# Tangent sums to rows: a product with a centring matrix, in two parts, in place of transposes and a row mean

## The chip, the cores and the metric

The kernel runs on one core of a Trainium2 chip. The metric is the device time of one execution in microseconds (us), given as the median of several runs. Below, PE is TensorE, DVE is VectorE, ACT is ScalarE, POOL is GpSimd, and SP is the engine whose queue issues the loads.

## What is computed

Four graph layers run one after the other on x (4096 rows of 64) and a dense 0/1 matrix adj (4096 by 4096, fp32). Each is followed by a residual and a layer norm. Layer 0 is a mean over neighbours with a linear map, layer 2 a weighted sum over the last 100 neighbours, and layers 1 and 3 are hyperbolic attention. Of these, layer 3 cut to its core (layer 1 is alike but for constants):

```
x_tan = _logmap0(x)
x_local = _logmap(x[:, None, :], x[None, :, :])
logits = (x_tan @ w_l)[:, None] + (x_tan @ w_r)[None, :] + att_b[0]
adj_att = sigmoid(logits) * adj
support_t = einsum('ij,ijd->id', adj_att, x_local)
return _proj(_expmap(x, support_t))
```

The kernel never forms x_local. For a row i the sum over j comes out as a combination of x_i and of sums over j of a weight times a row that depends on j alone. These last sums are the "tangent sums" of this document. The rows that go into them carry a multiple of their scale in every one of their 64 columns, so that the sum of a result row over its 64 columns gives the total weight, and the row less its own mean gives the part along the x_j.

## The kernel before

**Tiling.** 4096 rows are 32 blocks of 128 (`NB`), and 4 groups of 1024 (`NW`, `GROUPS`, taken from 3 down to 0). A group is eight blocks (`WB`). Every pass over adj goes group by group; within a group, 16 loads `g` of 1 MB bring two blocks each.

**Attention (`attend`, L914).** For each of the two blocks of a load, PE makes scores `zp` for 1024 columns (L935, L938, L941), ACT makes `sig` (L943) and `sq` (L946), DVE multiplies (L949), then once for both blocks DVE does L951, and PE adds up into `acc` (L955). After 16 loads ACT copies `acc` to `sums` (L962): 128 partitions by 512 columns. The 128 partitions are two halves of 64 features, the first for the group's rows 0 to 511, the second for rows 512 to 1023.

**Moving the rows (`move`, L972).** For each group, `move` turns `sums` to rows (`to_rows_of`: four fp32 PE transposes, L969, into one PSUM tile `aux`), ACT copies them to `of` (the buffer named `z0`, L985), DVE sums each row (`sum_1`, L988), divides by 64 (L989), and subtracts the mean, which gives `u` (L991). POOL multiplies x by `u` (L992), ACT squares `u` (L994), and DVE sums both over the row (L999, L997). Then follows a chain of some fifty DVE operations on 128 by 8 numbers (L1001 to L1065, with three reciprocal square roots of ten operations each, L673 to L679), and at the end `u` and x are scaled (L1068, and L1067 on POOL) and added to give the next layer's rows (L1071). In layer 3, `store` writes these rows out (L1407, issued from ACT's queue); after layer 1, `linear` turns them into the supports of layer 2 (L1081 to L1103).

**What sets the order.** `move`, `linear`, `prepare` and `store` are generators: each `yield n` hands back the turn for n ticks, and the passes call `tick` once or more for every block. `near()`, `soon()` and `after(n)` give such waits; in layers 1 and 3 each of them is one tick, in layer 2 `near()` is one, `soon()` none and `after(12)` three. The main queue takes `behind` of the group before and then `move` of this group. So the `move` of a group runs during the pass of the next group; that of group 0 of layer 1 runs during the first pass of layer 2, and that of group 0 of layer 3 after all passes. The program order so made is then list-scheduled, with each engine running its own list in order, except in layers 0 and 2, where the order on PE and ACT stays as written (`manual_schedule`, `FIXED`).

**Buffers.** `take` hands out one of two PSUM tiles named `aux` (one bank each), shared by `move`, `linear`, `prepare` and `spread_left`; `free` makes a generator wait in program order while one is in use. Tiles from `grp` and `nums` have one buffer for each name: a second `move` can write `u` only when L1071 of the first has read it.

Of the kernel before, what the change touches and what calls it, by code (L numbers as in the profile page):

```python
# [10 lines left out]
F32 = mybir.dt.float32  # L11
# [4 lines left out]
ALU = mybir.AluOpType  # L16
AX = mybir.AxisListType
PSUM = bass.MemoryType.PSUM

P = 128  # L20
N = 4096
D = 64
# [9 lines left out]
WB = WW // P  # L32
# [26 lines left out]
def gnn_stack_kernel(  # L59
# [15 lines left out]
    nc = tc.nc  # L75
    V = nc.vector
# [3 lines left out]
    ident = const.tile([P, P], F32, name="ident")  # L80
# [488 lines left out]
    def stream(fits):  # L569

        with ExitStack() as st:

            def pool(name, bufs=1, **kw):
                return st.enter_context(tc.tile_pool(name=name, bufs=bufs, **kw))

            keep = pool("f_keep")
            xs = pool("f_xs", 2)
            loads = pool("f_loads", 6)
            row = pool("f_row")
# [10 lines left out]
            queues, place, done, held = ([], []), [0, 0], set(), []  # L590
# [27 lines left out]
            def soon():  # L618


                return 0 if place[0] in (0, 2) else 1

            def after(small):


                each = {0: 1.6, 2: 6.0}.get(place[0])
                return 1 if each is None else 1 + int(small / each)

            def near():

                return 3 if place[0] == 0 else 1

            def take(dtype, *shape):

                held.append(1)
                return aux.tile(list(shape), dtype, name="aux")

            def free():
                while held:
                    yield 1  # L640
# [3 lines left out]
            def x_of(layer):  # L644

                if layer not in layers_x:
                    layers_x[layer] = xs.tile([P, NB, D], F32, name="x")
                return layers_x[layer]
# [10 lines left out]
            def grp(name, bufs=None):  # L659
                kw = {"bufs": bufs} if bufs else {}  # L660
                return row.tile([P, WB, D], F32, name=name, **kw)

            def nums(name, n=WB):
                return row.tile([P, n], F32, name=name)

            def over(v):
                return v[:, :, None].to_broadcast([P, v.shape[1], D])
# [29 lines left out]
            V.memset(turn, ROOT + OFF)  # L697

            ys = keep.tile([P, WB, 3 * D + 10], F16, name="ys")
            yd = keep.tile([P, WB, D + 10], F16, name="yd")
# [2 lines left out]
            for k in range(3):  # L705
                part = float(np.float16(rest))
# [258 lines left out]
            def to_rows_of(sums):  # L965

                t = take(F32, P, SB, 2, D)
                for k in range(SB):
                    nc.tensor.transpose(t[:, k], sums[:, k * P : (k + 1) * P], ident)  # L969
                return t.rearrange("p k h f -> p h k f")  # L970

            def move(layer, s, sums, curve):  # L972
# [4 lines left out]
                least = 1e-15 if layer == 1 else 1e-30  # L977
                at = blocks(s)
                xg, x2g = x_of(layer)[:, at, :], x2[:, at]
                sum_1, k, d, uu = nums("sum_1"), nums("k"), nums("d"), nums("uu")  # L980
                u, w, sq, of = grp("u"), grp("w_att"), grp("sq"), grp("z0")
                yield from free()
                t = to_rows_of(sums)
                yield near()
                nc.scalar.copy(of.rearrange("p (h k) f -> p h k f", h=2), t)  # L985
                held.pop()
                yield near()
                V.tensor_reduce(sum_1, of, AX.X, ALU.add)  # L988
                V.tensor_scalar(k, sum_1, 1.0 / D, None, ALU.mult)  # L989
                yield soon()  # L990
                V.tensor_sub(u, of, over(k))  # L991
                nc.gpsimd.tensor_mul(w, xg, u)  # L992
                yield after(12)
                nc.scalar.activation(sq, u, AF.Square)  # L994
                yield near()
                yield soon()
# [27 lines left out]
                y2, xy, den, p, q = (nums(n) for n in ("y2", "xy", "den", "p", "q"))  # L1024
# [16 lines left out]
                px, qd, w2, t = nums("px"), nums("qd"), nums("w2"), nums("mt")  # L1041
# [85 lines left out]
            with ExitStack() as lp:  # L1127
# [85 lines left out]
                with tc.manual_schedule(engines=FIXED):  # L1213
                    for s in GROUPS:
                        sums = [ps.tile([P, W], F32, name="acc") for _ in range(2)]
                        counts = [ps.tile([P, W], F32, name="acc") for _ in range(2)]
                        parts = ((first, sums, P), (third, counts, D + 1))
                        for g in reversed(range(NB // 2)):
# [5 lines left out]
                            for k in (1, 0):  # L1224
                                j = 2 * g + k
                                for lhs, accs, m in parts:
                                    for h in range(2):
# [3 lines left out]
                                            start=j == BLOCKS[0], stop=j == BLOCKS[-1],  # L1231
                                        )
                            if g == s * WB // 2 + 1:

                                for lhs, accs, m in parts:
                                    for h in range(2):
                                        for k in range(SB):
# [3 lines left out]
                                                start=False, stop=False,  # L1241
# [24 lines left out]
            def attention(layer, curve, rates, behind):  # L1266

                need((layer, GROUPS[0]))
                for n, s in enumerate(GROUPS):
                    if n:  # L1270
                        need((layer, s, "left"))
                    then = GROUPS[n + 1] if n + 1 < NW else None
                    sums = attend(layer, s, rates[n], then)
                    move_s = move(layer, s, sums, curve)
                    if n:
                        last = n + 1 == NW
                        later(in_turn((layer + 1, s + 1), behind(s + 1)), last, 9 * last)
                    later(move_s)
                    if n + 1 == NW:
                        later(in_turn((layer + 1, s), behind(s)))  # L1280
# [113 lines left out]
            with tc.manual_schedule(engines=FIXED):  # L1394

                for some in (GROUPS[:2], GROUPS[2:3], GROUPS[3:]):
                    accs = wide_pass(some) if len(some) == 2 else narrow_pass(some[0])
                    for s, acc in zip(some, accs):
                        sums = row.tile([P, W], F32, name="sums", bufs=2)
# [15 lines left out]
            t, g = nums("m1", 1), nums("g1", 1)  # L1415
# [4 lines left out]
            sq = row.tile([P, D], F32, name="w_sq")  # L1420
# [16 lines left out]

    fits = const.tile([P, 1], F32, name="fits")
    stream(fits)

    n_fit = const.tile([1, 1], I32, name="n_fit")
    with tc.tile_pool(name="fit_ps", bufs=1, space=PSUM) as ps:
        t = ps.tile([1, P], F32, name="fit_t")
# [52 lines left out]
```

## Time and profile before

| | |
|---|---|
| median of 3 runs | 1151.56 us (1148.69 to 1153.72) |
| the profiled execution | 1150.32 us, span 1148.8 us |
| PE, DVE, ACT, POOL busy | 1012.6, 964.3, 820.6, 60.3 us |
| granted PE clock, mean | 0.969 |
| HBM read | 269.55 MB, 236 GB/s over the span |
| attention groups of layer 1 (copies of `sums`) | 281.3, 364.4, 451.0, 539.2 us |
| attention groups of layer 3 (copies of `sums`) | 868.2, 951.5, 1033.8, 1114.7 us |
| passes of layer 2 (first copy of their sums) | 643.3, 706.1, 777.1 us |

The span is the time from the first to the last instruction in the profile of one execution; the time of that execution is 1.5 us longer. The copies of `sums` mark the ends of the groups, so that one reads off how long a group lasts: 82.3 us from 951.5 to 1033.8. The busy time of PE is modelled from the starts of its matmuls, so a PE that is 88% busy isn't at 88% of its peak. A mean over the span hides stages with different limits: the document goes by stage.

### The profile page before, as it was taken

The numbers are of one execution on the slowest core, as the hardware profiler recorded it, in microseconds if no ns is written. First come the engines' busy times: TensorE is split into PE (matmuls) and PEld (weight loads), VectorE is DVE, ScalarE is ACT, GpSimd is POOL, SyncE is SP. The second block draws the span as 40 slices with busy tenths as digits, with TensorE's granted clock in tenths as the row PEclk, the third lists the DMA queues.
The fourth block names the chain that finished last, engine by engine and source line by source line (L and its number), as shares of the span: only waits on it lengthen the run. The fifth ranks groups of instructions, "written<-read, shape, count | busy, mean of one in ns | idle before, by whom it ended". The sixth has DMA issues, their size and how long they took to land.

```text
span 1148.8 us, 13484 instructions
## 1 busy us (share of the span) xinstructions
PE 1012.6 (88%) x4832; PEld 386.9 (34%) x4917; DVE 964.3 (84%) x1901; ACT 820.6 (71%) x886; POOL 60.3 (5%) x97
## 2 busy tenths in 40 slices
PE   6999897899899999988999987898898999999870
PEld 3445544233333333332333232233333333233320
DVE  5687898999999899989773476529998999999996
ACT  0003215899889788976767778888998998889850
POOL 0020120000000000000000020000000000000001
PEclk9999998999999999999999999899999999999995
DMA  9999998556566466644988976686465666566400
GB/s 344 421 381 400 373 417 329 193 176 218 176 210 218 164 209 210 220 169 140 323 297 312 341 268 235 220 278 235 150 217 183 220 218 204 204 210 206 149 1 21
DMA packets 38418, 271.57 MB, mean 236 GB/s; under 512 B 4550, under 2 KB 4550, under 8 KB 5574
## 3 DMA queue, kind: packets, MB, share of 16 engines
q1 hardware_dynamic: 37440, 269.50, 65.3%
q10 hardware_dynamic: 902, 1.12, 0.3%
q8 instruction: 40, 0.66, 0.2%
q14 instruction: 36, 0.29, 0.1%
HBM read 269.55 MB, written 1.05 MB: 236 GB/s over the span
## 4 chain that ended last, share of the span: by engine, by line
DVE 57%; PE 26%; ACT 7%; DMA 4%; issue 3%; POOL 2%; SPq 0%; ACTq 0%; POOLq 0%
DVE t L951 20%; DVE t L949 20%; PE z L1372 8%; PE acc L1387 5%; PE acc L955 4%; DMA edges<-in_adj_dram 4%; PE acc L1229 3%; DVE junk L741 2%; ACT sq L946 2%; ACT sq L1381 2%; PE z L935 1%; PE z L938 1%; POOL sq L768 1%; PE aux L842 1%; PE z L941 1%
## 5 line engine op out<-in xcount | busy, mean ns | idle before, releaser
L943 ACT ACTIVATE sig<-left_b,right 128x1024 f32<-128x1024 f32 x256 | 293.8, 1149 | 45.9 <-DVE t L949 35.0
L949 DVE SCALAR_TENSOR_TENSOR t<-z,sig 128x1024 f32<-128x1024 f32 x256 | 309.9, 1216 | 13.9 <-ACT sq L946 12.9
L946 ACT ACTIVATE sq<-z,turn 128x1024 f32<-128x1024 f32 x256 | 281.5, 1106 | 27.3 <-PE z L941 25.1
L951 DVE SCALAR_TENSOR_TENSOR t<-sq,t 128x2048 f32<-128x2048 f32 x128 | 292.9, 2289 | 0.7
L955 PE MATMUL acc<-t,xe 128*64 128x512 f32 x1024 | 260.2, 619 | 32.3 <-DVE t L951 28.7
L935 PE MATMUL z<-edges,two_i 128*128 128x512 bf16 x465 | 183.1, 394 | 19.7 <-DVE t L949 19.5
L938 PE MATMUL z<-lo_hi,hi_lo 128*128 128x512 f16 x512 | 194.1, 379 | 3.2
L941 PE MATMUL z<-dst,src 74*128 74x512 f16 x512 | 195.1, 381 | 0.0
L1381 ACT ACTIVATE sq<-z,at_edge 128x512 bf16<-128x512 f32 (+1 forms) x192 | 152.6, 829 | 51.3 <-PE z L1372 47.9
L955 PEld LDWEIGHTS acc<-t,xe 128*64 128x64 f32 x1024 | 64.0, 138 | 168.5 <-DVE t L951 88.4
L741 DVE SCALAR_TENSOR_TENSOR t<-edges 128x2048 bf16<-128x2048 f32 x32 | 73.9, 2311 | 38.5 <-DMA edges<-in_adj_dram 37.5
L1372 PE MATMUL z<-edges,pass_by 128*128 128x512 bf16 x241 | 87.5, 400 | 17.3 <-ACT sq L1381 15.8
L935 PEld LDWEIGHTS <-two_i 128*128 128x128 bf16 x512 | 50.3, 98 | 142.7 <-issue 97.7
L1229 PE MATMUL acc<-edges,first 128*128 128x512 bf16 x241 | 77.4, 397 | 21.4 <-DMA edges<-in_adj_dram 20.7
L1387 PE MATMUL acc<-sq,halves 128*64 128x512 bf16 x512 | 82.0, 398 | 5.7 <-ACT sq L1381 3.5
L1372 PE MATMUL z<-edges,enter 128*128 128x512 bf16 x240 | 85.1, 397 | 0.1
L1229 PE MATMUL acc<-edges,third 128*65 128x512 bf16 x256 | 80.9, 398 | 0.6
L741 DVE SCALAR_TENSOR_TENSOR junk<-edges 128x2048 bf16<-128x2048 f32 x32 | 73.2, 2286 | 5.1 <-DMA edges<-in_adj_dram 4.8
L938 PEld LDWEIGHTS <-hi_lo 128*128 128x128 f16 x512 | 50.3, 98 | 67.9 <-issue 23.7
L941 PEld LDWEIGHTS <-src 74*128 74x128 f16 x512 | 49.4, 96 | 69.2 <-issue 4.0
L1229 PEld LDWEIGHTS <-first 128*128 128x128 bf16 x256 | 24.3, 98 | 50.2 <-issue 22.6
L1387 PEld LDWEIGHTS <-halves 128*64 128x64 f16 x512 | 18.9, 108 | 63.0 <-issue 62.7
(260 smaller groups left out, 758.3 us busy)
## 6 DMA issues: line engine op xcount, KB each, us to landing
edges<-in_adj_dram SPq DMA_DIRECT2D x256, 1024.0 KB, 4.9
x<-in_x_dram SPq DMA_DIRECT2D x4, 256.0 KB
out_dram<-x ACTq DMA_DIRECT2D x4, 256.0 KB, 4.0
w_sb<-in_L_gnn_W_dram ACTq DMA_DIRECT2D x1, 32.0 KB, 4.8
given<-in_L_gnn_b_dram ACTq DMA_DIRECT2D x1, 0.2 KB
given<-in_L_gnn_bias_dram ACTq DMA_DIRECT2D x1, 0.2 KB
given<-in_L_gnn_b_att_dram ACTq DMA_DIRECT2D x1, 0.0 KB
given<-in_L_gnn_att_b_dram ACTq DMA_DIRECT2D x1, 0.0 KB
```

What stands on the lines that cost most here:

```text
L741: V.scalar_tensor_tensor(junk, a, 0.0, a, ALU.not_equal, ALU.not_equal, accum_out=odd[:, n : n + 1])
L935: nc.tensor.matmul(half, two_i, edge[:, at : at + W], start=True, stop=False)
L938: nc.tensor.matmul(half, hi_lo[:, of], lo_hi[:, to], start=False, stop=False)
L941: nc.tensor.matmul(half, src[:, of], dst[:, to], start=False, stop=True)
L943: nc.scalar.activation(sig, left_b, AF.Sigmoid, bias=right[:, j : j + 1])
L946: nc.scalar.activation(sq[:, k], zp, AF.Square, bias=turn, scale=-1.0 / UNIT)
L949: V.scalar_tensor_tensor(t[:, k], zp, 0.0, sig, ALU.max, ALU.mult)
L951: V.scalar_tensor_tensor(t, sq, HIGH**2, t, ALU.add, ALU.mult)
L955: nc.tensor.matmul(acc[h * D : (h + 1) * D, :], xe[:, j, :], t[:, k, h * W : (h + 1) * W], start=j == BLOCKS[0], stop=j == BLOCKS[-1],)
L1229: nc.tensor.matmul(accs[h][:m], lhs[:, j, :], edge[:, at : at + W], start=j == BLOCKS[0], stop=j == BLOCKS[-1],)
L1372: nc.tensor.matmul(z[:, h : h + W], lhs, rhs[:, h : h + W], start=j == BLOCKS[0], stop=True, skip_group_check=True,)
L1381: nc.scalar.activation(w, z[:, :n], AF.Exp, bias=at_edge, scale=-LN2)
```

## The change

A constant `centre` (128 by 2 by 65) is made once. For half h, its rows h*64 to h*64+63 hold, in columns 0 to 63, the identity less 1/64, and in column 64 ones; all else is zero. A product of 128 columns of `sums` (as the stationary operand) with `centre` gives, for 128 rows of each half, the row less its mean and, in the 65th column, its sum. Four such products make a group. Each has 2 x 65 = 130 output columns[...]: they are done in two parts of two, each with its own `aux` tile and its own ACT copy. The copies write `all_u` (named `u_1`, 65 columns a row), of which `u` and `sum_1` are now views. The transposes, the copy to `of`, the row sum, the division and the subtraction are gone from `move`, and one `yield after(12)` ahead of the square. `to_rows_of` stays in use in `end_2`.

```diff
@@ setup @@
+            centre = keep.tile([P, 2, D + 1], F32, name="centre")
+            V.memset(centre, 0.0)
+            for h in range(2):
+                of = slice(h * D, (h + 1) * D)
+                V.tensor_scalar(
+                    centre[of, h, :D], ident[of, of], -1.0 / D, None, ALU.add
+                )
+                V.memset(centre[of, h, D:], 1.0)
@@ move @@
-                sum_1, k, d, uu = nums("sum_1"), nums("k"), nums("d"), nums("uu")
-                u, w, sq, of = grp("u"), grp("w_att"), grp("sq"), grp("z0")
-                yield from free()
-                t = to_rows_of(sums)
-                yield near()
-                nc.scalar.copy(of.rearrange("p (h k) f -> p h k f", h=2), t)
-                held.pop()
-                yield near()
-                V.tensor_reduce(sum_1, of, AX.X, ALU.add)
-                V.tensor_scalar(k, sum_1, 1.0 / D, None, ALU.mult)
-                yield soon()
-                V.tensor_sub(u, of, over(k))
+                k, d, uu = nums("k"), nums("d"), nums("uu")
+                w, sq = grp("w_att"), grp("sq")
+
+                all_u = row.tile([P, WB, D + 1], F32, name="u_1")
+                u, sum_1 = all_u[:, :, :D], all_u[:, :, D]
+                for part in range(2):
+                    yield from free()
+                    t = take(F32, P, 2, 2, D + 1)
+                    for i in range(2):
+                        cols = slice((2 * part + i) * P, (2 * part + i + 1) * P)
+                        nc.tensor.matmul(t[:, i], sums[:, cols], centre, start=True, stop=True)
+                    yield near()
+                    nc.scalar.copy(
+                        all_u.rearrange("p (h k) f -> p k h f", h=2)[:, 2 * part : 2 * part + 2], t
+                    )
+                    held.pop()
+                    yield near()
                 nc.gpsimd.tensor_mul(w, xg, u)
-                yield after(12)
                 nc.scalar.activation(sq, u, AF.Square)
                 yield near()
                 yield soon()
```

## The prediction

> **What bounds the kernel now.** I read the chain of work that ended last first, then engine busy time by stage, then the operations that the change touches, then DVE's timeline where they stand, and the table of waits.
>
> ```profile
> DVE 57%; PE 26%; ACT 7%; DMA 4%; issue 3%; POOL 2%; SPq 0%; ACTq 0%; POOLq 0%
> ...
> 540.00:645.00 105.00, 101.70 (x539) 33.84 (x548) 59.40 (x175) 73.19 (x76) 4.41 (x3) 1.00 0.85 301
> ...
> 952.00:1034.00 82.00, 76.99 (x326) 26.57 (x330) 80.57 (x116) 72.04 (x71) 2.32 (x2) 0.98 0.61 207
> ...
> 1115.00:1149.00 34.00, 0.93 (x5) 0.50 (x5) 21.04 (x116) 1.72 (x4) 4.38 (x3) 0.55 0.05 19
> ```
>
> The columns of a stretch are its length, then busy us of PE, weight loads, DVE, ACT, POOL. In an attention group of layer 3 (952 to 1034) DVE is busy 80.57 of 82.00 us: it is the bound, and PE (76.99) is close. In the first pass of layer 2 (540 to 645) PE is busy 101.70 of 105.00 and DVE is not the bound. From 1115 on only one chain of small DVE operations is left.
>
> ```profile
> L985 ACT COPY z<-aux x8: 572/574/586, 282.8 to 1116.0; 128x512 f32<-128x512 f32 x8
> ...
> L988 DVE TENSOR_REDUCE sum<-z x8: 676/678/686, 283.8 to 1116.7; 128x8 f32<-128x512 f32 x8
> ...
> L991 DVE TENSOR_TENSOR u<-z,k x8: 679/686/694, 285.7 to 1124.3; 128x512 f32<-128x512 f32 x8
> ...
> L969 PE MATMUL aux<-ident,sums x48: 270/273/329, 282.0 to 1115.7; 128*128 128x128 f32 x48
> ...
> L992 POOL TENSOR_TENSOR w_att<-x,u x8: 1263/1276/1284, 286.5 to 1125.1; 128x512 f32<-128x512 f32 x8
> ```
>
> Eight moves, one for each group of two layers. Their start times give the places: six lie inside attention groups (283, 397, 503, 871, 954 and 1036 us), one in layer 2 (559), one in the tail (1117). Of the 48 transposes 32 are the moves'; `end_2` keeps 16.
>
> ```profile
> 974.36 0.68 DVE L1071 TENSOR_TENSOR x<-u,w_att 128x512 f32<-128x512 f32 x1
> 974.96 1.22 DVE L949 SCALAR_TENSOR_TENSOR t<-z,sig 128x1024 f32<-128x1024 f32 x1
> 976.09 0.68 DVE L991 TENSOR_TENSOR u<-z,k 128x512 f32<-128x512 f32 x1
> 976.69 1.22 DVE L949 SCALAR_TENSOR_TENSOR t<-z,sig 128x1024 f32<-128x1024 f32 x1
> ...
> 1115.65 0.17 DVE L677 TENSOR_TENSOR rs_t<-n 128x8 f32<-128x8 f32 x1
> 1116.65 0.69 DVE L988 TENSOR_REDUCE sum<-z 128x8 f32<-128x512 f32 x1 [0.83 <-ACT z L985]
> 1117.26 0.16 DVE L678 SCALAR_TENSOR_TENSOR rs_t<-rs_t,mt 128x8 f32<-128x8 f32 x1
> ...
> 1123.54 0.69 DVE L1071 TENSOR_TENSOR x<-u,w_att 128x512 f32<-128x512 f32 x1 [0.93 <-POOL w_att L1067]
> 1124.26 0.69 DVE L991 TENSOR_TENSOR u<-z,k 128x512 f32<-128x512 f32 x1
> ```
>
> Two things to see. In the loop L991 takes 0.60 us of DVE, start to start. And `u` has one buffer: L991 of a move runs only after L1071 of the move before it, although its L988 ran long before (954 against 976; 1116.65 against 1124.26). In the tail L988 sits in the middle of the older move's square root and holds it from 1115.82 to 1117.26.
>
> ```profile
> DVE d L999 <- POOL w_att L992: 8.6, 6, 1.5
> ...
> ACT sq L994 <- DVE u L991: 9.2, 2, 8.4
> ```
>
> After L991, DVE stands still for POOL's product, about 1.4 us in six of the eight moves (four of them in the loop).
>
> **What the Trainium skill says.** (1) FP8 and Floating Point Precision, TensorE Precision Notes: a true fp32 product takes four passes. The trace agrees: the fp32 products of L1186 and L1187, 65 columns each, stand 0.111 us apart (two records, 0.056 us each), and 4 x 65 columns at the 2.4 GHz that TensorE: Matmul & The Clock Gate gives in its opening table are 0.108. (2) SBUF — State Buffer, Who interferes with whom: a DVE instruction with two SBUF inputs and a GpSimd instruction that reads SBUF block each other for a whole instruction. It agrees: POOL's L768 takes 1.04 us alone and 2.95 to 3.11 beside DVE's L741. (3) VectorE: DVE Perf Modes, Mode 1×: this mode asks nothing of strides. So a `u` with rows 65 apart should cost L1068 and L1071 nothing; no row before shows it.
>
> **The change, part by part.**
>
> *Removed from DVE.* L988 (0.60 us start to start), L989 (0.08 to 0.17; I take 0.10) and L991 (0.60): 1.30 us a move. In the six loop moves that is work of the bound engine: 6 x 1.30 = 7.8 us gained. In layer 2 PE is the bound: nothing.
>
> *PE.* Four transposes (0.11 us apart, 0.44 in all) become four fp32 products of 130 columns: twice L1186's 0.111 us, 0.22 each, 0.89 in all, 0.45 more a move. Lower end: nothing more; upper end: 0.96 more, if each part also shows the 0.27 us of a lone matmul. What hides it: late in an attention group the scores of the second block are ready at 1097.14 (end of L941) and DVE takes them at 1098.33, 1.2 us later. That cover is good in the dense groups of layer 3 (moves at 954 and 1036). At the other four group changes DVE does wait for ACT's L946 and that for PE's L941 (1.45 us at 299.03, 2.37 at 394.54, 2.39 at 506.39), so I charge 4 x 0.45 = 1.8 us. Without any cover it would be 2.7.
>
> *ACT.* One copy of 512 columns (0.574) becomes two of 260. The nearest row, L1102 with 256 columns out of PSUM, takes 0.379: 0.76, or 0.19 more. ACT is busy 72.04 of 82.00 us there; I charge nothing (1.1 us over six moves without cover).
>
> *Ticks.* In layers 1 and 3 the square (L994) stays four ticks after the start (two `near`, `soon`, `after` against four `near`). In layer 2 it comes after four instead of five.
>
> *Wait moved to ACT.* The copies now write the single `u_1` themselves, so ACT, no longer DVE, waits for L1071 of the move before. Behind them on ACT stand the next L943 and L946, and DVE waits for those. In the loop of layer 3 the copies must lie about 975 and 1076, where ACT has gaps (1.17 us before 976.21); I take nothing. Both `aux` buffers are held meanwhile (952 to 975), so `spread_left` (L910 at 960) moves to about 977; it is needed at 1034. In layer 2, where ACT's order is written out, L985 ran at 555.58, but L1071 ends at 556.88: with the copy (0.38) the next L1381 starts about 1.1 us late, and PE behind it about 1.0. In exchange ACT's 0.82 us wait for L991 goes, which had cost PE 0.60. With PE's own 0.45: a loss of 0.9 us.
>
> *POOL.* L992 now waits for ACT; POOL has nothing queued behind. DVE no longer stops for it right after L991, so the four 1.4 us stalls in the loop can vanish (5.6 gained); or L992 collides with L951, which has two SBUF inputs, and holds it 1.3 us (4 x 1.3 = 5.2 lost). I take a quarter of the gain, 1.4 us.
>
> *Tail.* The stall at L988 goes: 1.44 us, and 0.1 for L989. After L1071 (end 1124.23) POOL started at 1125.10; now two copies of 0.38, overlapping by about 0.09, and a handover: about 0.80 instead of 0.87. 1.5 us gained. If the store's DMA issue (0.34 on ACT) goes ahead of them, 1.2.
>
> *Set-up.* Five small DVE operations for `centre`, 0.06 to 0.22 each as their like at 0.9 to 9.3 us, in all about 0.6: DVE waits 2.67 us for the first x there. Nothing; 0.6 without that cover. SP's loads are not touched, and DMA is at 0.61 in these groups.
>
> *Sum:* -7.8 + 1.8 + 0.9 - 1.4 - 1.5 = -8.0 us. Against the profiled execution, 1150.32 us (span 1148.8 and 1.5 around it), that is 1142.3; this execution is 1.24 below the median of 1151.56, so for the median 1143.5.
>
> **Rivals.**
>
> *Half the gain.* The group changes are bound by PE and ACT, not DVE. For it: the waits named at 299, 394 and 506. Then only the two dense moves and the tail count: -2.6 - 1.5 + 0.9 = -3.2, about 1148.4. Against it: even those stretches begin with DVE operations in a row.
>
> *More than forecast.* All four POOL stalls vanish, 4.2 us beyond the quarter taken: 1139.3. For it: the two dense moves (L991 at 976 and 1077) have other work ahead of L999 and no stall already. Against it: L951 next to L992.
>
> *Slower.* ACT is stopped in order by the single `u_1`. If, in layer 3, the copies stand one pair of blocks too early in ACT's queue, ACT is held a full cycle (4.75 us, L951 to L951) and the pipeline then refills (PE's scores 2.64 and L946 1.11): 8.5 us at each of two places, 17 us, 1160.5. It decides from some 14 us of such ACT waits on. For it: ACT did wait for DVE in order in layer 2 and the tail (L994, L1020). Against it: no such wait in the loop.
>
> **How the numbers follow.** Forecast 0.58 (1139 to 1147.5, of which 0.10 above 1145.8); half the gain 0.20; more 0.10; slower 0.12 (0.10 beyond 1157.3). 0.5%, 5.8 us, is about what a measurement of this kernel can tell from no change. So faster 0.58, same 0.32, slower 0.10. Leaving out the far half of the low case and the slower one, the range is 1138 to 1154.
>
> **What would show it.** Right: DVE's busy time in a layer 3 group down by about 1.3 and the group shorter by as much; ACT copies waiting for L1071 only in layer 2 (about 1.3 us) and the tail; no L988 in the tail, and a tail 1.5 us shorter; PE records of the product 0.11 us apart. Wrong: DVE less busy with the group as long (PE or ACT bound), L951 above 2.29 us beside L992, or ACT idle before the copies in the loop.

## The result, and the profile after

The changed kernel takes 1143.13 us (median of 15 runs, 1137.66 to 1148.34), the kernel before, run beside it, 1151.75 us (15 runs, 1147.20 to 1154.66). The ratio is 0.9923, with a 95% interval of 0.9907 to 0.9939: 0.8% faster, 8.6 us between the medians. The prediction was 1143.5. The profiled execution takes 1140.81 us, with a span of 1139.1 (before: 1150.32 and 1148.8).

The total came as forecast. The places did not. Lines have moved by 10 to 14: L949 and L951 are now L959 and L961, L946 is L956, the product is L1000 and its copies L1002, POOL's product L1007, the row sums L1011 and L1013, the end of a move L1079 to L1085. The table gives the time from one copy of `sums` to the next.

| us | before | after | difference | predicted, about |
|---|---|---|---|---|
| layer 1, three groups with a move | 83.1, 86.6, 88.2 | 81.2, 86.3, 86.9 | -3.5 | -3.6 |
| layer 2, first pass | 104.1 | 104.0 | -0.1 | +0.9 |
| layer 3, three groups with a move | 83.3, 82.3, 80.9 | 81.2, 81.1, 84.6 | +0.4 | -3.8 |
| tail | 34.1 | 26.0 | -8.1 | -1.5 |

The last column puts the terms of the prediction where they belong: a loop move is 1.30 us off DVE, and in the four that aren't in the dense groups 0.35 us of stalls goes and 0.45 us of PE comes. The rows add up to -11.3 us, the span to -9.7: the other +1.6 lies in layer 0 with the first group of layer 1, the last two passes of layer 2 and the first group of layer 3, which differ by 1 to 3 us (the first of them by up to 5) between kernels with the same code there.

The chain of work that ended last, of the changed kernel:

```profile
DVE 53%; PE 29%; ACT 8%; DMA 6%; POOL 2%; issue 2%; ACTq 0%; SPq 0%; POOLq 0%; DVEq 0%
```

DVE's share is down from 57% and PE's is up from 26%. The next view is the busy time by stretch, of the three groups of layer 3 and the tail (its columns as in the prediction; the number in brackets counts instructions, and the last three columns are the granted PE clock, the share of DMA and GB/s):

```profile
866.20:947.40 81.20, 77.08 (x338) 26.92 (x336) 79.82 (x119) 72.74 (x72) 1.31 (x1) 1.00 0.61 208
947.40:1028.50 81.10, 77.01 (x338) 26.96 (x336) 79.97 (x114) 72.70 (x73) 4.88 (x2) 1.00 0.62 211
1028.50:1113.10 84.60, 76.16 (x318) 25.49 (x315) 82.71 (x147) 66.67 (x66) 3.07 (x2) 0.96 0.35 122
1113.10:1139.10 26.00, 1.50 (x9) 1.05 (x9) 15.88 (x87) 2.05 (x5) 4.29 (x3) 0.57 0.07 24
```

The same stretches before:

```profile
868.20:951.50 83.30, 77.93 (x329) 26.87 (x334) 80.23 (x115) 72.86 (x72) 1.27 (x1) 0.98 0.60 204
951.50:1033.80 82.30, 77.29 (x327) 26.67 (x331) 80.87 (x116) 72.34 (x71) 2.32 (x2) 0.98 0.61 207
1033.80:1114.70 80.90, 73.44 (x308) 24.72 (x311) 80.59 (x131) 66.41 (x64) 2.32 (x2) 0.98 0.37 127
1114.70:1148.80 34.10, 0.93 (x5) 0.50 (x5) 21.31 (x117) 2.01 (x4) 4.38 (x3) 0.55 0.05 19
```

A move has three DVE instructions fewer, yet two of the three groups have more of them than before (119 and 147), and the tail has 30 fewer. Work has changed place. Over these four stretches DVE is busy 258.4 us instead of 263.0 and idle 14.5 instead of 17.6: of the 7.7 us that layer 3 gains, 4.6 are DVE's work and 3.1 its idle time. In the three groups of layer 1 DVE is busy 1.1 us more than before (245.9 against 244.8), since operations have come in there too (the first pass of layer 2 has 141 DVE instructions instead of 175); the 3.5 us gained are idle time alone.

The operations concerned, and two lines from the table of waits (total us, times, longest):

```profile
L1002 ACT COPY u<-aux x16: 358/378/382, 281.4 to 1116.4; 128x260 f32<-128x260 f32 x16
L1007 POOL TENSOR_TENSOR w_att<-x,u x8: 1178/1306/3324, 282.2 to 1116.9; 128x512 f32<-128x512 f32 x8
...
L1085 DVE TENSOR_TENSOR x<-u,w_att x8: 675/686/693, 371.4 to 1133.8; 128x512 f32<-128x512 f32 x8
```

```profile
DVE d L1013 <- POOL w_att L1007: 7.3, 5, 3.5
...
ACT u L1002 <- DVE x L1085: 3.4, 2, 2.5
```

The copies take the 0.38 us expected, and `u` in rows 65 apart costs L1085 nothing (0.686 against 0.683 us for L1071). ACT waits for L1085 twice, 2.5 us in the tail and 0.9 inside the second group of layer 3:

```profile
954.74 0.66 ACT L1002 COPY u<-aux 128x260 f32<-128x260 f32 x2 [0.87 <-DVE x L1085]
```

In layer 2 it doesn't wait for L1085, which starts there at 544.7, six us ahead of the first copy (550.74). DVE still stands still for POOL's product, 7.3 us in all. In the six attention groups with a move that wait is 5.7 us before and after. What has gone there is DVE's waits for ACT's scores (`sq`, L946): 9.0 us before, 1.2 after.

Now the start of a group of layer 3, DVE's timeline (start, duration):

```profile
869.85 0.69 DVE L1013 TENSOR_REDUCE d<-w_att 128x8 f32<-128x512 f32 x1 [1.07 <-POOL w_att L1007]
870.45 1.22 DVE L959 SCALAR_TENSOR_TENSOR t<-z,sig 128x1024 f32<-128x1024 f32 x1
871.58 0.68 DVE L1011 TENSOR_REDUCE uu<-sq 128x8 f32<-128x512 f32 x1
...
872.43 0.17 DVE L1016 TENSOR_TENSOR k<-k,rb 128x8 f32<-128x8 f32 x1
872.63 0.17 DVE L1019 TENSOR_TENSOR kx<-k,x 128x8 f32<-128x8 f32 x1
872.83 0.17 DVE L1020 SCALAR_TENSOR_TENSOR t<-d,kx 128x8 f32<-128x8 f32 x1
872.91 0.16 DVE L1024 TENSOR_TENSOR xt<-d,kx 128x8 f32<-128x8 f32 x1
```

The same place before:

```profile
875.44 0.23 DVE L1001 SCALAR_TENSOR_TENSOR k<-d,k_c,sum 128x8 f32<-128x8 f32 x1
875.70 0.17 DVE L1002 TENSOR_TENSOR k<-k,rb 128x8 f32<-128x8 f32 x1
875.79 1.22 DVE L949 SCALAR_TENSOR_TENSOR t<-z,sig 128x1024 f32<-128x1024 f32 x1
```

Two things are to be seen. Small operations that need each other's results stand 0.20 us apart when they follow one another (872.43, 872.63, 872.83), but one whose follower doesn't need it takes only 0.08 or 0.09, be the follower long (875.70 to 875.79) or small (872.83 to 872.91). And the changed kernel does eleven of them in a row here, which the kernel before spread out one by one.

A third thing neither the prediction nor the experiments looked at. At the same group change before:

```profile
870.86 1.94 PE L955 MATMUL acc<-t,xe 128*64 128x512 f32 x8
...
879.85 3.60 PE L955 MATMUL acc<-t,xe 128*64 128x512 f32 x8 [1.31 <-DVE t L951]
```

```profile
876.40:879.80 3.40, 1.48 (x6) 0.48 (x5) 3.40 (x4) 2.80 (x5) 0.00 (x0) 1.00 0.21 36
879.80:883.20 3.40, 3.35 (x8) 0.77 (x8) 3.40 (x4) 2.60 (x3) 0.00 (x0) 0.50 0.65 272
```

```profile
886.06 1.23 DVE L949 SCALAR_TENSOR_TENSOR t<-z,sig 128x1024 f32<-128x1024 f32 x1 [1.52 <-ACT sq L946]
```

PE has stood still for DVE (1.74 and 1.31 us) and is busy 1.48 of 3.40 us. In the next 3.4 us its granted clock is 0.50, the same eight products take 3.60 us instead of 1.94, the scores behind them come late, and DVE waits 1.52 us. Two more such stretches, at 292.7 and 982.2, come just ahead of waits of 1.45 and 1.27 us, so that 4.2 of the 9.0 us of DVE's waits for `sq` stand behind half clock. (Stretches in the last 5 us of a group are left out of this count.) After the change there is one (1038.4), with no such wait behind it. Without the ticks of the later experiments, every traced first group of layer 1 or 3 with the old `move` has this stretch (six of them), and none of the twelve with the new products has it. No experiment changed the clock alone, so what it is worth isn't shown.

Last, the tail:

```profile
1115.37 0.69 DVE L1085 TENSOR_TENSOR x<-u,w_att 128x512 f32<-128x512 f32 x1 [0.93 <-POOL w_att L1081]
...
1118.09 0.69 DVE L1013 TENSOR_REDUCE d<-w_att 128x8 f32<-128x512 f32 x1 [0.58 <-POOL w_att L1007]
```

```profile
1116.15 0.38 ACT L1002 COPY u<-aux 128x260 f32<-128x260 f32 x1 [2.50 <-DVE x L1085]
...
1134.52 0.34 ACTq L1421 DMA_DIRECT2D out_dram<-x  x1
```

The older move's last operation (L1085) starts 2.3 us after the last copy of `sums`, at 1115.37; before, it was L1071, 8.8 us after it (1123.54 against 1114.7). So of the tail's 8.1 us, 6.6 lie ahead of POOL's last product (3.8 us after the copy of `sums`, before 10.4), 0.1 between it and the issue of the last store, and 1.4 in that store's transfer (4.6 us to the end of the span, before 5.9), which no instruction of the change touches.

### The profile page after: what moved, and what is told of

It is laid out like the page before. It is cut to its first block, busy times and chain, and to the rows that moved or that the text cites. A ratio compares the mean times of both kernels' runs of the same rounds, so it can differ in the third digit from the quotient of the medians.

```text
span 1139.1 us, 13626 instructions
## 1 busy us (share of the span) xinstructions
PE 1021.6 (90%) x4949; PEld 391.2 (34%) x4949; DVE 956.0 (84%) x1882; ACT 821.2 (72%) x894; POOL 66.1 (6%) x97
## 4 chain that ended last, share of the span: by engine, by line
DVE 53%; PE 29%; ACT 8%; DMA 6%; POOL 2%; issue 2%; ACTq 0%; SPq 0%; POOLq 0%; DVEq 0%
DVE t L959 21%; DVE t L961 20%; PE z L1386 10%; DMA edges<-in_adj_dram 6%; PE acc L1401 5%; PE acc L1243 4%; PE acc L965 2%; ACT sig L953 2%; ACT sq L956 2%; ACT sq L1395 1%; PE aux L1106 1%; PE aux L852 1%; PE z L945 1%; DVE junk L751 1%; PE z L951 1%
## 5 line engine op out<-in xcount | busy, mean ns | idle before, releaser
L959 DVE SCALAR_TENSOR_TENSOR t<-z,sig 128x1024 f32<-128x1024 f32 x256 | 310.0, 1216 | 5.9 <-ACT sq L956 5.0
L956 ACT ACTIVATE sq<-z,turn 128x1024 f32<-128x1024 f32 x256 | 281.5, 1106 | 22.8 <-PE z L951 20.7
L961 DVE SCALAR_TENSOR_TENSOR t<-sq,t 128x2048 f32<-128x2048 f32 x128 | 292.9, 2288 | 0.7
L965 PE MATMUL acc<-t,xe 128*64 128x512 f32 x1024 | 255.2, 611 | 28.5 <-DVE t L961 24.4
L945 PE MATMUL z<-edges,two_i 128*128 128x512 bf16 x512 | 201.7, 394 | 21.5 <-DVE t L959 21.5
L951 PE MATMUL z<-dst,src 74*128 74x512 f16 x512 | 195.2, 381 | 0.0
L965 PEld LDWEIGHTS acc<-t,xe 128*64 128x64 f32 x1024 | 63.6, 137 | 163.0 <-DVE t L961 85.9
L1243 PE MATMUL acc<-edges,first 128*128 128x512 bf16 x256 | 80.6, 396 | 20.0 <-DMA edges<-in_adj_dram 19.8
L1386 PE MATMUL z<-edges,enter 128*128 128x512 bf16 x256 | 90.8, 397 | 0.0
L951 PEld LDWEIGHTS <-src 74*128 74x128 f16 x512 | 49.2, 96 | 67.5 <-issue 2.3
L1081 POOL TENSOR_TENSOR w_att<-x,p 128x512 f32<-128x512 f32 x8 | 12.9, 1615 | 495.0 <-DVE q L1079 495.0
```

The costliest lines, as they stand in the source:

```text
L945: nc.tensor.matmul(half, two_i, edge[:, at : at + W], start=True, stop=False)
L951: nc.tensor.matmul(half, src[:, of], dst[:, to], start=False, stop=True)
L956: nc.scalar.activation(sq[:, k], zp, AF.Square, bias=turn, scale=-1.0 / UNIT)
L959: V.scalar_tensor_tensor(t[:, k], zp, 0.0, sig, ALU.max, ALU.mult)
L961: V.scalar_tensor_tensor(t, sq, HIGH**2, t, ALU.add, ALU.mult)
L965: nc.tensor.matmul(acc[h * D : (h + 1) * D, :], xe[:, j, :], t[:, k, h * W : (h + 1) * W], start=j == BLOCKS[0], stop=j == BLOCKS[-1],)
```

## The experiments

Two theories stood at first. The **work theory** is the prediction's: DVE is the bound, and each 1.3 us taken off it shortens the loop. The **order theory** was formed on the table above: what counts is where the chains of small operations stand, because one costs 0.20 us in the tail and 0.08 among long operations, and the change only brings them forward. A third came later, the **stop theory**: each group change has a stop of DVE, set by how long it takes from `sums` to the next thing DVE can do, and everything on that way counts in full.

All ratios are to the kernel before in runs beside it (1151.2 to 1151.8 us). Sums over a layer are compared where work can shift between its stages: "layer 1" is three groups (before 257.9, after 254.4), "layer 3" three groups and the tail (before 280.6, after 272.9). Each layer sum comes from one trace, and the same code can differ: layer 1 with the new lines takes 254.4 us in the changed kernel and 256.1 in experiment 4, where a stretch of half clock (from 490.3) lies ahead of a wait of 1.4 us. Differences under 2 us in one trace show little. Of the older move's DVE operations, 62 stood behind the last L951 of layer 3 before, and 142 in all up to the last L1071; after the change it is 25 and 106.

In the kernels of the experiments some lines stand one or two further on (the product L1001 for L1000, and so on).

**1. The work put back, off the chain.**

```diff
+                again, ka = grp("z0"), nums("ka")
+                V.tensor_reduce(ka, u, AX.X, ALU.add)
+                V.tensor_scalar(ka, ka, 1.0 / D, None, ALU.mult)
+                V.tensor_sub(again, u, over(ka))
                 nc.gpsimd.tensor_mul(w, xg, u)
```

> The changed kernel, with a row sum, a division and a subtraction of the old size put back on DVE in every move, on results that nobody reads: DVE's work is that of before, but nothing of the move waits for it. Work theory (the gain is the 1.3 us of DVE work taken out of each move where DVE is the bound): about 7.8 us of the six loop moves come back, so about 1150 us. Order theory (the gain is that the move chains start earlier and get further inside the attention groups, which empties the tail): the tail after the last copy of the sums stays near 26 us and the time stays at 1144 to 1147 us.

Measured: 1144.21 us, ratio 0.9940 (0.9918 to 0.9961). Layer 1 stays at 254.2, layer 3 is 277.0 instead of 272.9.

```profile
944.10:1027.30 83.20, 78.52 (x338) 27.48 (x337) 81.96 (x121) 72.97 (x72) 2.74 (x2) 0.98 0.57 204
1027.30:1113.10 85.80, 76.21 (x318) 25.54 (x315) 83.92 (x150) 66.58 (x65) 3.08 (x2) 0.96 0.34 120
1113.10:1140.10 27.00, 1.53 (x9) 1.05 (x9) 17.20 (x90) 2.08 (x5) 4.29 (x3) 0.56 0.07 23
```

The total spoke for the order theory, but the layers tell more. In layer 3 the four moves cost 4.1 us, near the 5.2 that the work theory asks for, but not evenly: nothing in the first group (81.0 against 81.2, where the added work partly fills the wait for POOL's product), 2.1 and 1.2 in the others, 1.0 in the tail. In layer 1 three moves cost nothing: the last operation of the third starts at 549.9 instead of 544.7, inside the first pass of layer 2, which takes in 173 DVE instructions instead of 141 and hardly gets longer (104.6 against 104.0). What is added to DVE there pushes the chain into a stage that PE bounds.

**2. Two buffers.** `u_1` and `w_att` get a second buffer, so that a move need not wait for L1085 of the one before.

```diff
-                w, sq = grp("w_att"), grp("sq")
+                w, sq = grp("w_att", 2), grp("sq")
-                all_u = row.tile([P, WB, D + 1], F32, name="u_1")
+                all_u = row.tile([P, WB, D + 1], F32, name="u_1", bufs=2)
```

> The changed kernel with two buffers each for u_1 and w_att, so that a move's copies no longer wait for the last addition of the move before. Both theories: the 2.5 us wait of ACT in the tail and the 0.9 us in layer 2 go. Work theory: nothing else, 1141 us, 2 us below the changed kernel. Order theory: in layer 3 the moves of groups 2 and 1 also start 5 to 14 us earlier in their groups, so their chains get further and the time falls by 3 to 6 us, to 1137 to 1140 us.

Measured: 1139.55 us, ratio 0.9893 (0.9871 to 0.9915). Layer 3 is 269.2: groups of 81.2, 80.6 and 81.5 us and a tail of 25.9. The time is the order theory's, but its interval reaches the work theory's 1141. The 84.6 us group is gone, so its length came from a chain that started late.

**3 and 4. One layer alone.** The new lines run in layer 3 only, or in layer 1 only; the other layer keeps the old ones.

> The new move in layer 3 alone, the old one in layer 1. Work theory: three loop moves of 1.3 us and 1.5 us of tail, so 5.4 us below before, 1146 us. Order theory: the tail falls from 34 to about 26 us as in the changed kernel, the groups of layer 3 give nothing in sum, 7 to 8 us below before, 1144 us.

Measured: 1141.67 us, ratio 0.9917 (0.9893 to 0.9941); layer 3 is 273.0, layer 1 258.1. This is below both forecasts.

> The new move in layer 1 alone, the old one in layer 3. Work theory: three loop moves of 1.3 us less 0.9 us in layer 2, 3 us below before, 1148.7 us. Order theory: the tail stays at 34 us; at most what the groups of layer 1 show, 3.5 us, less what layer 2 and the first group of layer 3 lost in the profile of the changed kernel (2.9 us), so 0 to 2 us below before, 1150 to 1152 us.

Measured: 1148.69 us, ratio 0.9983 (0.9971 to 0.9996); layer 1 is 256.1, layer 3 279.5. The number is the work theory's, but by experiment 1 not for its reason. Layer 1 alone gives 2.5 us (0.5 to 3.3); on top of layer 3 nothing of it is seen, since layer 3 alone is as fast as the whole change (1141.67 against 1143.13).

**5. Two buffers in the kernel before.**

```diff
-                u, w, sq, of = grp("u"), grp("w_att"), grp("sq"), grp("z0")
+                u, w, sq, of = grp("u_1", 2), grp("w_att", 2), grp("sq"), grp("z0")
```

> Nothing of the change is in it: the kernel before, with two buffers each for u and for POOL's product w_att, so that a move need not wait for L1071 of the move before. All DVE work of L988, L989 and L991 and the transposes stay. In the order written for DVE, 25 of the older move's operations are left behind the last pair of blocks of layer 3 instead of 62 (as in the changed kernel), and 108 in all up to the last row sum instead of 142. Order theory (the gain is where the chains of small operations stand, and the single u puts them late): the tail falls from 34.1 to about 27 us, the last group of layer 3 grows by up to 4, the whole is 1144 to 1147. Work theory (the gain is 1.3 us of DVE work a move): nothing is gained, 1150 to 1152.

Measured: 1147.65 us, ratio 0.9973 (0.9961 to 0.9985): between the two forecasts.

```profile
951.00:1034.10 83.10, 75.95 (x328) 26.52 (x331) 83.10 (x125) 72.73 (x71) 4.90 (x2) 1.00 0.58 205
1034.10:1118.10 84.00, 73.79 (x308) 24.84 (x311) 83.45 (x150) 66.03 (x64) 4.32 (x2) 0.98 0.34 122
1118.10:1146.10 28.00, 0.93 (x5) 0.50 (x5) 16.89 (x89) 2.01 (x4) 4.38 (x3) 0.56 0.06 22
```

The tail falls by 6.1 us with no work removed, as the order theory said. But the two groups ahead of it take in the operations that left it (125 and 150 instead of 116 and 131) and grow by 0.8 and 3.1. Layer 3 gains 2.3 in all. So most of what leaves a tail comes back in a group.

**6. Plain transposes in two parts.**

```diff
-                        nc.tensor.matmul(t[:, i], sums[:, cols], centre, start=True, stop=True)
+                        nc.tensor.transpose(t[:, i], sums[:, cols], ident)
```

> The changed kernel with plain transposes in two parts in place of the products; it leaves out the centring and takes 1 for the row sums, so L988, L989 and L991 are absent from DVE as in the changed kernel, and PE has 0.45 us a move less to do. But the order written for DVE has the chains late again: 55 of the older move's operations are left behind the last pair of blocks, 136 in all (before: 62 and 142; changed: 25 and 106). Order theory: a tail of 32 to 33 us, whole 1147 to 1150. Work theory: at least as fast as the changed kernel, 1141 to 1143.

Measured: 1134.48 us, ratio 0.9857 (0.9829 to 0.9884). The tail is long again, 30.5 us, and no kernel here is faster: the groups of layer 3 take 79.8, 79.8 and 79.9 us, layer 3 is 270.0 and layer 1 251.1. That refutes the order theory as the account of the whole. Something at the group changes is worth more than the place of the chains. It isn't the products' time on PE alone: by the scale of experiment 7 that is about 3 us, and layers 1 and 3 are 6.2 us shorter than in the changed kernel. Here one copy instead of two stands ahead of the next L956 on ACT, too, and no stretch of half clock falls into these groups (but for the last 2.4 us of one); the shares aren't shown.

**7. The products three times over.**

```diff
+                        for _ in range(3):
                             nc.tensor.matmul(t[:, i], sums[:, cols], centre, start=True, stop=True)
```

> The changed kernel with each of the four products of a move done three times over (same result): 1.78 us more of PE a move, by the 0.11 us between records. The order of DVE behind the last pair is that of the changed kernel (25 and 106). If PE's time at a group change is on the path, as the prediction charged for four of the six moves and in the tail: 4 x 1.78 + 1.8 + about 1.8 in layer 2, or some 10 us more, 1153. If it lies beside other work in the loop, only the tail and layer 2 grow, 1.8 us each: about 1146 to 1147.

Measured: 1156.33 us, ratio 1.0048 (1.0030 to 1.0066), 13 us above the changed kernel. Layer 1 is 258.8 (+4.4 for 3 x 1.78 = 5.3 us of PE), layer 3 is 280.0 (+7.1 for 4 x 1.78 = 7.1). ACT's timeline at a group change, and the wait behind it:

```profile
871.33 0.57 ACT L972 COPY sums<-acc 128x512 f32<-128x512 f32 x1
...
873.62 0.38 ACT L1003 COPY u<-aux 128x260 f32<-128x260 f32 x1 [0.67 <-PE aux L1001]
877.02 0.38 ACT L1003 COPY u<-aux 128x260 f32<-128x260 f32 x1 [3.02 <-PE aux L1001]
877.29 1.12 ACT L956 ACTIVATE sq<-z,turn 128x1024 f32<-128x1024 f32 x1
```

```profile
DVE d L1014 <- POOL w_att L1008: 19.9, 6, 4.8
```

This is the stop theory's evidence. The copies stand ahead of the next L956 in ACT's queue and of POOL's product, and DVE's reads of that product stand ahead of its next long operation. So the products' time holds ACT, then POOL, then DVE: DVE's wait for POOL grows from 7.3 to 19.9 us. That this is nearly the 13 us lost is partly chance. The first group changes of the two layers have 3.7 us of the growth each, the other two of layer 1 have 3.0 in all, and 2.2 fall into layer 2, whose first pass grows by 1.8. The second and third groups of layer 3 have no such wait and are still 1.7 and 3.1 us longer; the third has 6.8 us of half clock (from 1050.2) where the changed kernel has 3.4. PE's order changed as well: at 873.96 eight products L965 (1.94 us) stand between the two parts. So one for one is the sum over the layer, and not the law of each group change.

**8. One part.** The 65th column is split off: four products of 128 columns and four of 2, one copy of 512 columns and one of 8.

```diff
-                    t = take(F32, P, 2, 2, D + 1)
+                t = take(F32, P, SB, 2, D)
+                s1 = take(F32, P, SB, 2)
...
+                nc.scalar.copy(u.rearrange("p (h k) f -> p k h f", h=2), t)
+                nc.scalar.copy(sum_1.rearrange("p (h k) -> p k h", h=2), s1)
```

> The changed kernel with the 65th column split off: four products of 128 columns into one PSUM bank and four of 2 columns for the sums into another, copied as one of 512 and one of 8 columns. The order of DVE behind the last pair is that of the changed kernel (25 and 106). ACT's large copy takes 0.57 us again and ends later than the second of two of 0.38, the small one some 0.2. If the two parts are worth something, it is the start of POOL's product: 0.1 to 0.3 us in the tail; otherwise nothing: 1142 to 1145 in either case, and the tail 26.0 to 26.6.

Measured: 1147.63 us, ratio 0.9966 (0.9952 to 0.9979): slower than the 1142 to 1145 expected, by half of the change's gain. The tail, at 26.1 us, is as expected. Layer 3 is 277.2.

```profile
863.64 0.57 ACT L972 COPY sums<-acc 128x512 f32<-128x512 f32 x1
...
866.14 0.59 ACT L1003 COPY u<-aux 128x512 f32<-128x512 f32 x1 [0.89 <-PE aux L1000]
866.62 0.17 ACT L1004 COPY u<-aux 128x8 f32<-128x8 f32 x1
866.68 1.13 ACT L956 ACTIVATE sq<-z,turn 128x1024 f32<-128x1024 f32 x1
```

With one part ACT waits 0.89 us for the last product, and L956 starts 3.04 us after the copy of `sums`; in the changed kernel it is 2.11 (866.21 to 868.32), with plain transposes, where the second copy comes after L956, 1.77. The three groups of layer 3 are longer than the changed kernel's by 0.8, 1.8 and 1.6 us (the third with 6.8 us of half clock, from 1039.0, instead of 3.4).

**9 to 11. The moves later in the group.** Six ticks of waiting put the products among the scores of the first pairs of blocks, where other work stands ready. With two buffers:

```diff
                 all_u = row.tile([P, WB, D + 1], F32, name="u_1", bufs=2)
+                yield 6 if place[0] != 2 else 0
```

> The changed kernel with two buffers for u_1 and w_att, and six ticks of waiting ahead of each move of layers 1 and 3, so that the products stand among the scores of the first pairs of blocks of the next group instead of behind its third block. If the products' time at a group change is on the path (as the run with threefold products suggests), it now lies beside DVE's work and the first reads of POOL's product no longer stand in a row: the groups of layer 3 take 80.0 to 80.5 us instead of 81.2, 80.6 and 81.5, those of layer 1 lose about 1 us each; the tail has 31 of the older move's operations left instead of 15 and is 28 to 29 us instead of 25.9. Whole: 1136 to 1139. If PE at the group change were not on the path, it would be no faster than the kernel with two buffers alone, 1139.5 to 1142.

Measured: 1135.47 us, ratio 0.9868 (0.9846 to 0.9889). Layer 1 is 250.4; layer 3 is 270.3, with groups of 79.4, 81.4 and 82.3 us (two of them longer than forecast) and a tail of 27.2. DVE's timeline at a group change:

```profile
871.58 2.29 DVE L961 SCALAR_TENSOR_TENSOR t<-sq,t 128x2048 f32<-128x2048 f32 x1
874.94 0.69 DVE L1014 TENSOR_REDUCE d<-w_att 128x8 f32<-128x512 f32 x1 [1.07 <-POOL w_att L1008]
875.55 2.35 DVE L959 SCALAR_TENSOR_TENSOR t<-z,sig 128x1024 f32<-128x1024 f32 x2
```

The stop for POOL is still there, but no run of small operations follows it. With the move of the last pass not delayed (`and not (layer == 3 and s == 1)`):

> As the kernel with six ticks of waiting and two buffers, but the move that runs in the last pass of layer 3 isn't delayed, so that 17 of its operations are left behind the last pair instead of 31. The tail is 26.2 us, the last group 81.5: in all 1135.5 to 1138, or the same as with the delay everywhere if an operation moved from the tail into a group in a run of dependent ones costs there what it costs in the tail.

Measured: 1136.15 us, ratio 0.9864 (0.9843 to 0.9886): no different. The tail is 24.8 us and the group ahead of it 83.2, where the run with the delay everywhere had 27.2 and 82.3. And with single buffers, so that only the ticks are added to the changed kernel:

> The changed kernel with six ticks of waiting ahead of each move of layers 1 and 3, and with single buffers. The chains are late in layer 3 as in the kernel before (65 of the older move's operations behind the last pair, 146 in all; before 62 and 142), though all of L988, L989 and L991 are gone. Tail 32 to 34 us as before, the groups of layer 3 80 us each, those of layer 1 about 1 us shorter than in the changed kernel: 1139 to 1142. If all that counts were how early the chains stand, it would be near the kernel before, 1147 to 1150.

Measured: 1139.42 us, ratio 0.9905 (0.9886 to 0.9924).

```profile
861.60:941.00 79.40, 76.50 (x333) 27.40 (x336) 77.87 (x101) 72.43 (x72) 2.76 (x1) 1.00 0.59 212
941.00:1021.90 80.90, 76.69 (x333) 27.23 (x337) 79.77 (x113) 72.75 (x73) 3.09 (x2) 1.00 0.60 216
1021.90:1101.90 80.00, 72.69 (x312) 25.09 (x315) 78.73 (x117) 66.47 (x66) 3.09 (x2) 1.00 0.34 124
1101.90:1135.40 33.50, 1.53 (x9) 1.05 (x9) 22.80 (x137) 2.16 (x5) 4.30 (x3) 0.55 0.05 19
```

This is the clearest page of the study. Layer 3 takes 273.8 us, the changed kernel 272.9, and yet the tail is as long as in the kernel before and the groups are short. What the changed kernel has in its groups this one has in its tail. So the tail that is 8.1 us shorter isn't needed for the gain.

**12. The control.** The kernel before with the six ticks.

> The kernel before with six ticks of waiting ahead of each move of layers 1 and 3 and nothing of the change: the control for the changed kernel with the same wait (single buffers), which took 1139.4. DVE keeps L988, L989 and L991; 69 of the older move's operations stand behind the last pair, 149 in all (the other: 65 and 146). If DVE's work is what the change takes away, that kernel is faster than this one by 1.3 us at each of six group changes and 1.5 in the tail, 9 us: this one 1147 to 1150. If the gain of the wait and the gain of the change are the same one (a shorter stop at the group change), this one is near 1140 to 1143.

Measured: 1151.24 us, ratio 0.9997 (0.9977 to 1.0017). Against the kernel above, which differs from it by the change alone, that is 11.8 us. Layer 3's three groups are 79.4, 82.2 and 82.7, in sum 4.0 us more for three moves of 1.3 us, though not move by move (0, 1.4 and 2.7 us); its tail is 2.4 more, of which 1.6 come after its last addition (L1071). Layer 1 is 250.5, no more than the other's 250.3. But the first pass of layer 2 is 108.1 us instead of 104.0:

```profile
553.00 1.11 ACT L1382 ACTIVATE sq<-z,at_edge 128x1024 bf16<-128x1024 f32 x1 [0.45 <-PE z L1373]
557.60 0.63 ACT L995 ACTIVATE sq<-u 128x512 f32<-128x512 f32 x1 [3.49 <-DVE u L992]
558.14 2.10 ACT L1382 ACTIVATE sq<-z,at_edge 128x1024 bf16<-128x1024 f32 x2
```

Here the late chain of layer 1 holds ACT in its fixed order for 3.49 us, and PE behind it for 3.27 us (to 559.28), and PE's granted clock is 0.50 in the 3.4 us from 559.0. The ticks alone do nothing; the change is worth as much with them as without, or more.

## Why the prediction was right in its sum and wrong in its places

The sum fits partly by luck. Against the forecast of each place, the tail gained 6.6 us more and layer 2 1.0 more; the groups of layer 3 gained 4.2 less, and 1.6 us were lost in stages that the forecast put at nothing. Two of the signs it named spoke against it: DVE's busy time in the groups of layer 3 fell by 0.4 and 0.9 us and then rose by 2.1, where 1.3 less was asked for, and ACT stood idle ahead of the copies inside a group (0.87 us).

**DVE's 1.30 us a move, 7.8 us in six loop moves: about right over layer 3, wrong in layer 1.** In layer 3 putting the work back costs 4.1 us for four moves (experiment 1), and taking it away under the ticks gives 4.0 in three groups (12), in neither case anything in the first of the groups. In layer 1 both say nothing, 0.2 us either way. Its three groups did become 3.5 us shorter, near the forecast, but not by DVE's work, since the kernel with that work back has the same 254.2. The step that failed is "in the six loop moves that is work of the bound engine". It was read from a group's busy time, and that busy time didn't fall: over the six groups it went from 486.5 to 488.4 us, and what shrank was DVE's idle time. The step leaves out that other operations move in, that work added at a group change can fall into a wait, and that the last chain of layer 1 runs over into layer 2, so work saved in layer 1 first brings that chain forward.

**Tail -1.5: measured -8.1, the term most wrong.** The prediction saw "only one chain" from 1115 on; there were two, with 62 operations of the older move behind the last L951, and it took them as fixed. They were not: with L988, L989 and L991 out of the chain's head, each move ends earlier, the next begins earlier because of the single `u`, and 62 leftover operations became 25. But the groups ahead took them in, the last one at 3.7 us more than before. That they cost nearly as much there, in runs, as in the tail is a reading that no run isolates; the kernel before with two buffers fits it, with nearly the same tail and 2.3 us gained in the layer. Over layer 3 the forecast was -5.3 us and the measurement -7.7, of which 4.6 are DVE's busy time and 3.1 its idle time; experiments 1 and 5 give 4.1 for the work and 2.3 for the order. That these add up is not shown.

**PE's 0.45 us, charged at four of six moves, "that cover is good in the dense groups of layer 3": wrong.** The products themselves take what was forecast, eight records 0.11 us apart (from 866.96 to 867.74). But tripling them cost as much as PE's added time in layer 3, and four fifths of it in layer 1. By that scale the change's own 0.45 us would cost about 2.9 us in the seven moves of layers 1 and 3 (11.5 us for 12.4 of PE, times 3.15), not 1.8; this is an estimate, since the scale holds order and clock as well. The cover was looked for between PE and DVE late in a group. At the first change of a layer there is none: copies, POOL's product and DVE's reads follow in order.

**ACT's copies at no cost: wrong for the same reason.** A later copy delays L956 and, through it, DVE: 0.93 us later with one part, and 0.8 to 1.8 us a group. The second part of the change, "in two parts", is thus worth up to half of its gain (4.5 of 8.6 us; the kernel with one part also has four small products more), although it seems to be there only because four products would have more columns (520) than the largest fp32 `aux` tile in these traces (512).

**POOL's stalls, a quarter of 5.6 us gained in the loop: not seen.** There they are 5.7 us before and after; the fall from 8.6 to 7.3 us lies in layer 2 and the tail. The waits for `sq`, which the prediction used as bounds of PE's cover and left as they were, fell from 9.0 to 1.2 us. The rival "half the gain" named just these waits, and so had the better picture of the group changes, but it expected them to stay. The feared collision came, but with the other party paying: L1007 started at 955.47, 0.02 us after an L961 of 2.29 us, and took 3.32 us, while L961 keeps its mean of 2.29. The Trainium skill has this in SBUF — State Buffer, Who interferes with whom: a DVE instruction with two SBUF inputs contends with a GpSimd instruction that reads SBUF, and the order of issue decides who is blocked. The trace agrees: the 1.18 us that the product takes alone, counted from L961's end at 957.74, give 958.92, and it ended at 958.79. Once DVE paid: L1082 at 464.28 took 1.53 us instead of 0.69 while POOL's L1081 ran until 465.26.

**Layer 2, +0.9: not seen.** The older chain ended ahead of the copies, so ACT didn't wait for L1085 there, and the pass took 104.0 us instead of 104.1.

**The slower rival** needed ACT stopped for a full cycle inside a group of layer 3. One stop came, of 0.87 us (954.74): with the chains earlier, `u` is free, or nearly so, when the copies come up.

**A version faster than both** is the changed kernel with two buffers and the ticks: 1135.5 us against 1151.5 before.

## What to carry to other kernels

When a chain of small operations is spread over several stages, account for it over all of them: what leaves one stage comes back in another, at a price that depends on whether the operations stand in a row or among long ones. A busy engine bounds a stage only if work can't run over into a stage that another engine bounds. Split a stage into an engine's busy and idle time before and after: that tells work taken away from waits taken away. At a change of stage follow each result through every queue that it stands in: time on PE or ACT that looks covered by the mean can count in full where the next engine's first instruction waits for it. And look at the granted clock just behind a stop, not only at its mean.

## What the hardware showed unexpectedly

Dependent operations of 128 by 8 numbers on DVE stand 0.20 us apart in a row (872.43, 872.63, 872.83), and one with an independent operation behind it takes 0.08 to 0.09. A POOL product of 128 by 512 takes 1.18 us in the tail, where DVE stands still (1.26 before, with the rows of `u` 64 apart; why isn't known), and 3.32 when it starts just behind a long DVE operation, without any cost to that operation. And PE's granted clock fell to 0.50 for 3.4 us after a stretch in which PE was busy 1.48 of 3.40 us, with two stops of 1.74 and 1.31 us at it; that the stops are the cause wasn't tested.
